# Seams between the first two layers of a four-layer image kernel: where the projection, the additions and a table load stand

## The chip, the cores and the metric

The kernel runs on one core of one Trainium2 chip. The core has five engines that matter here: TensorE (PE, matrix products, with its weight loads listed as PEld), VectorE (DVE), ScalarE (ACT), GpSimd (POOL) and SyncE (SP, which issues transfers). The metric is the device time of one execution in microseconds. All data is fp32.

## The reference

A batch of four images, 56 x 56 pixels with 128 channels, passes through four layers, each of the form `x = x + layer(groupnorm(x))`. The change touches layers 0 and 1 and the step between them:

```python
# layer 0: window attention, then full attention, then an MLP
xf = windows(x)                                     # 7 x 7 windows, shifted by 3, 4 heads
xf = xf + mha(layernorm(xf))                        # all 3136 pixels, 4 heads of 32, ends with @ wo + bo
h  = gelu(layernorm(xf) @ w1 + b1)                  # 128 -> 512
xf = xf + (h @ w2 + b2)                             # 512 -> 128
x  = x + xf
# layer 1: every pair of pixels of one image row
x_n      = groupnorm(x)
edge     = relu(x_n @ W1.T [i] + x_n @ W2.T [j] + be)   # 56 x 56 pairs of each row
x        = x + relu(concat(x_n, edge.sum(j)) @ Wn.T + bn)
```

Layers 2 (spectral attention) and 3 (a convolution with sums along rows) follow for all images together; they are not changed.

## The kernel before

The four images go through layers 0 and 1 one after the other (`first_layers` in `build`). Channels lie on the 128 partitions and the 3136 pixels on the free axis, in window order until the end of layer 0 (`xw` is the input, `xf` the running result) and in image order from then on (`x1`). For one image the steps are:

1. `fast_windows`: group norm, window attention, and the layer norm and q, k, v of the full attention.
2. `fast_attention`: the 3136 queries are worked off in 7 blocks of 448 (`blk(j)`). For each block the scores of 24 chunks of 128 keys and one of 64 are computed (L639, four heads in four 32-row strips of the array), exponentiated by ACT into a ring of slots (L641), summed by DVE (`f_acc`, L594) and multiplied with the values (L600). Score tiles alternate between two PSUM areas `s0` and `s1` (four and three banks). A list `late` delays the value products by two turns and the closing step `finish` by three, so that they stand behind scores of the next block. `finish(j)` takes one of the two PSUM areas (`pd`), lets PE sum the exponentials over the partitions (L607, L610), takes the reciprocal on DVE (L612) and writes the normalised block to `oT` (L613). PE's order in this stage is the order of the program text; that of the other engines is a scheduler's.
3. The output projection: seven matmuls with `wo`, all in one PSUM tile `po`, each followed by an addition to `xf` on DVE (L663, L664).
4. `mlp`: eight parts of 392 pixels. For all eight parts, PE centres the part (`m_pc`, L670), ACT squares it and copies it, PE averages the squares, ACT takes the root (L682) and DVE the reciprocal (L683) and the product (L868). Then, part by part, four matmuls and four Gelus make the hidden layer (L855, L856), one part ahead, four matmuls make the result `m_po` (L876, two PSUM banks in turn), DVE adds it to `xf` (L877), POOL adds `xw` and writes image rows of `x1` in three pieces (L883, L885, L886; two times three for the last part, whose rows wrap around), and DVE takes the statistics of those rows (L887). PE's order is that of the text here too.
5. `edge_layer`: `group_norm_factors` (L2320 to L2332) makes mean and factor, seven norms write `xg` (L192), and each of seven blocks of eight image rows is projected twice (`e_pa` L922, `e_pc` L924), evacuated by ACT (`evacuate`), combined in 14 turns of four pixels by DVE (`e_td`, L967) or by POOL and ACT (`e_tp`, L969, L971), added up by PE in `e_acc` (L974), and brought to the result (`output`, `finish`). The orders of PE, ACT and DVE are those of the text here.

Of the kernel before, what the change touches and what calls it, by code (L numbers as in the profile page):

```python
# [11 lines left out]
F32 = mybir.dt.float32  # L12
AF = mybir.ActivationFunctionType
ALU = mybir.AluOpType
# [4 lines left out]
P = 128  # L19
# [20 lines left out]
def blk(j):  # L40
    return slice(j * NB, (j + 1) * NB)
# [149 lines left out]
def apply_norm(k, out, xt, mr):  # L191
    k.nc.vector.tensor_scalar(out, xt, mr[:, 0:1], mr[:, 1:2], ALU.subtract, ALU.mult)  # L192
# [367 lines left out]
def fast_attention(k, w, xw, xf, mr):  # L560

    nc, tc = k.nc, k.tc
    scale = 1.0 / math.sqrt(32.0)
    heads = [slice(32 * h, 32 * h + 32) for h in range(4)]
    half = (slice(0, 64), slice(64, 128))
    with ExitStack() as es:  # L570
        big = es.enter_context(tc.tile_pool(name="f_big", bufs=1))
        qT = big.tile([P, TOK], F32, name="f_qT")
        kT = big.tile([P, TOK], F32, name="f_kT")
        va = big.tile([P, 25, P], F32, name="f_va")
        fast_windows(k, w, xw, xf, mr, qT, kT, va)

        ring = es.enter_context(tc.tile_pool(name="f_ring", bufs=1)).tile([P, RING, NB], F32, name="f_ring")
        wk = es.enter_context(tc.tile_pool(name="f_wk", bufs=2))
        ps = es.enter_context(tc.tile_pool(name="f_ps", bufs=1, space=PSUM))
        oT = es.enter_context(tc.tile_pool(name="f_out", bufs=1)).tile([P, TOK], F32, name="f_oT")  # L580
        late = []
        n = 0

        def bank(turn):
            return ps.tile([P, (4, 3)[turn], 512], F32, tag="s%d" % turn, name="f_s%d" % turn)

        def slots(j, c):
            s = (96 * j + 4 * c) % RING
            return ring[:, s:s + 4, :]

        def sums(j, c, acc):

            if 0 < c < SUMMED:
                nc.vector.tensor_add(acc, slots(j, 0) if c == 1 else acc, slots(j, c))  # L594

        def values(j, c, po, p24):
            for h in range(4):
                o = half[h % 2] if c == 24 else slice(0, P)
                p = p24[o, h // 2, :] if c == 24 else slots(j, c)[:, h, :]
                nc.tensor.matmul(po[heads[h], :NB], va[o, c, heads[h]], p, start=(c == 0), stop=(c == 24))  # L600

        def finish(j, raw, acc, p24, pd):

            for c in range(SUMMED - 1, 24):
                p = acc if c < SUMMED else slots(j, c)
                for h in range(4):
                    nc.tensor.matmul(pd[heads[h], 0, :NB], k.ones[:, 0:32], p[:, h, :], start=(c < SUMMED), stop=False)  # L607
            for h in range(4):
                o = half[h % 2]
                nc.tensor.matmul(pd[heads[h], 0, :NB], k.ones[o, 0:32], p24[o, h // 2, :], start=False, stop=True)  # L610
            den = wk.tile([P, NB], F32, name="f_den")
            nc.vector.reciprocal(den, pd[:, 0, :NB])  # L612
            nc.vector.tensor_mul(oT[:, blk(j)], raw, den)  # L613

        def flush(all_=False):

            nonlocal n
            if n % 2 and not all_:
                return
            while late and (all_ or late[0][0] < n):  # L620
                _, f, *a = late.pop(0)
                if f is finish:
                    a.append(bank(n % 2))
                    n += 1
                f(*a)

        with tc.manual_schedule(engines={mybir.EngineType.PE}):
            for j in range(NBLK):
                po = ps.tile([P, 512], F32, tag="po", name="f_po")
                raw = wk.tile([P, NB], F32, name="f_raw")  # L630
                acc = wk.tile([P, 4, NB], F32, name="f_acc")
                t, done = 0, 0
                while t < 96:
                    turn, slot = n % 2, (96 * j + t) % RING
                    m = min((4, 3)[turn], RING - slot, 96 - t)
                    ss = bank(turn)
                    for i in range(m):
                        c, h = divmod(t + i, 4)
                        nc.tensor.matmul(ss[:, i, :NB], kT[heads[h], c * P:(c + 1) * P], qT[heads[h], blk(j)],  # L639
                                         start=True, stop=True)  # L640
                    nc.scalar.activation(ring[:, slot:slot + m, :], ss[:, :m, :NB], AF.Exp, scale=scale)  # L641
                    t += m
                    while 4 * (done + 1) <= t:
                        sums(j, done, acc)
                        late.append((n + 2, values, j, done, po, None))
                        done += 1
                    n += 1
                    flush()
                ss = bank(n % 2)
                for h in range(4):  # L650
                    nc.tensor.matmul(ss[half[h % 2], h // 2, :NB], kT[heads[h], 24 * P:TOK], qT[heads[h], blk(j)],
                                     start=True, stop=True)
                p24 = wk.tile([P, 2, NB], F32, name="f_p24")
                nc.scalar.activation(p24, ss[:, 0:2, :NB], AF.Exp, scale=scale)
                late.append((n + 2, values, j, 24, po, p24))
                late.append((n + 2, nc.scalar.copy, raw, po[:, :NB]))
                late.append((n + 3, finish, j, raw, acc, p24))
                n += 1
                flush()
            flush(True)  # L660
        for j in range(NBLK):
            pm = ps.tile([P, 512], F32, tag="po", name="f_pf")
            nc.tensor.matmul(pm[:, :NB], w.wo, oT[:, blk(j)], start=True, stop=True)  # L663
            nc.vector.scalar_tensor_tensor(xf[:, blk(j)], pm[:, :NB], w.fbvo, xf[:, blk(j)], ALU.add, ALU.add)  # L664


def centre(k, pool, centred, src, squares, j):
# [171 lines left out]
def mlp(k, w, xf, xw, x1, st):  # L839
# [4 lines left out]
    with ExitStack() as es:  # L844
# [25 lines left out]
        for wi, ts in enumerate(parts):  # L870
            hT = ahead
            if wi < 7:
                ahead = hidden(parts[wi + 1])
            po = psum.tile([P, 512], F32, tag="acc", name="m_po")
            for f in range(4):
                nc.tensor.matmul(po[:, :N], w.w2[:, f, :], hT[:, f, :], start=(f == 0), stop=(f == 3))  # L876
            nc.vector.scalar_tensor_tensor(xf[:, ts], po[:, :N], w.b2, xf[:, ts], ALU.add, ALU.add)  # L877
            a = xf[:, ts].rearrange("p (w i j) -> p w i j", w=8, i=7)
            x = xw[:, ts].rearrange("p (w i j) -> p w i j", w=8, i=7)
            for i0, i1 in (((0, 7),) if wi < 7 else ((0, 4), (4, 7))):  # L880
                r0 = (7 * wi + 3 + i0) % HH
                rows = x1[:, r0:r0 + i1 - i0, :]
                nc.gpsimd.tensor_add(  # L883
                    rows[:, :, 3:52].rearrange("p i (w j) -> p w i j", w=7), a[:, 0:7, i0:i1, :], x[:, 0:7, i0:i1, :])
                nc.gpsimd.tensor_add(rows[:, :, 52:56], a[:, 7, i0:i1, 0:4], x[:, 7, i0:i1, 0:4])  # L885
                nc.gpsimd.tensor_add(rows[:, :, 0:3], a[:, 7, i0:i1, 4:7], x[:, 7, i0:i1, 4:7])  # L886
                nc.vector.bn_stats(st[:, wi + (i0 > 0), :], rows.rearrange("p l n -> p (l n)"))  # L887

# [3 lines left out]
def edge_layer(k, w, x1, st):  # L894
# [9 lines left out]
    with ExitStack() as es:  # L904
# [6 lines left out]

        mr = group_norm_factors(k, wk, bank, st)
        xg = big.tile([P, TOK], F32, name="e_xg")
        for j in range(NBLK):
            apply_norm(k, xg[:, blk(j)], xf[:, blk(j)], mr)
        ready = {}

        def project(j):
            if j >= NBLK:
                return  # L920
            pa = psum.tile([P, 512], F32, tag="pa", name="e_pa")
            nc.tensor.matmul(pa[:, :NB], w.W1, xg[:, blk(j)], start=True, stop=True)  # L922
            pc = psum.tile([P, 512], F32, tag="mm", name="e_pc")
            nc.tensor.matmul(pc[:, :NB], w.W2, xg[:, blk(j)], start=True, stop=True)  # L924
            ready[j] = pa, pc

        def evacuate(j):
# [21 lines left out]
            nc.vector.scalar_tensor_tensor(xf[:, blk(j)], po[:, :NB], w.nbn, xf[:, blk(j)], ALU.max, ALU.add)  # L949

        with tc.manual_schedule(engines={mybir.EngineType.PE, mybir.EngineType.Activation, mybir.EngineType.DVE}):
            for j in range(2):
                project(j)
                evacuate(j)
            last = None
            for j in range(NBLK):
# [4 lines left out]
                for g, e in enumerate(EDGE_TURNS):  # L961
# [18 lines left out]
                        evacuate(j + 1)  # L980
                    if g == 7 and last:
                        finish(last[0], po)
                    if g == 9:
                        nc.vector.tensor_reduce(rest, c[:, :, 0:nd], AX.X, ALU.add)
                sums = wk.tile([P, 4, NB], F32, name="e_sums")
# [1473 lines left out]
```

## Time and profile before

| What | Value |
|---|---|
| time, median of 3 runs | 3927.94 us (3925.56 to 3935.25) |
| span of the profiled execution | 3931.4 us |
| seven projections of the four images, PE (L663) | 56 passes, median 954 ns |
| additions on POOL (L883), four images | 36, median 907 ns |
| norms of layer 1 on DVE (L192, e_xg) | 28, median 505 ns |
| reciprocals of the layer norm in the MLP (L683), one image | 8, mean 2571 ns |

A line of the timeline gives the start, the duration, the engine, the source line and operation, the tile written and the tiles read with their shapes, and a count where equal instructions follow each other. The bracket says how long the engine stood idle before, and which instruction's end (engine, tile, line) ended that; "issue" means that no wait is visible. An fp32 matmul appears as two passes. Busy times of PE overlap, so a full PE is read from the absence of brackets rather than from its share.

### The profile page before, as it was taken

The page shows a single profiled execution, that of the slowest core. Times are in us where ns is not written, and L with a number is a line of the kernel's source. Part 1 is how long each engine was busy: PE and PEld are TensorE (multiplying, and loading weights), DVE is VectorE, ACT ScalarE, POOL GpSimd, SP SyncE. Part 2 cuts the span into 40 slices and gives each one's busy share as a digit, 9 for nine tenths or more (in the row PEclk, how much of TensorE's full clock was granted, in tenths as well). Part 3 has the DMA queues.
Part 4 walks back from the last instruction along what each step waited for, and adds up shares of the span by engine and source line. Part 5 has one row for each costly group of instructions (what it writes and reads, how often), then busy time and mean ns, then how long its engine had stood idle before and what let it go on. Part 6 is the DMA issues. An engine that isn't in the chain of part 4 may idle for free. (4 is left out here: it accounts for less than half of the span.)

```text
span 3931.4 us, 79382 instructions
## 1 busy us (share of the span) xinstructions
PE 3547.4 (90%) x35416; PEld 1589.8 (40%) x35416; DVE 2900.7 (74%) x2667; ACT 2048.0 (52%) x2055; POOL 1211.2 (31%) x671
## 2 busy tenths in 40 slices
PE   6899988989998898999889999998977979999988
PEld 4322234542223455222245532223446433336554
DVE  6588867758887685888769578885975867775664
ACT  4577754557775445877555467773522012215332
POOL 0000006600000570000047100001861869984665
PEclk8999999999999999999999999998978989999988
DMA  2000000000000000000000000000022048841101
GB/s 94 1 1 1 1 1 19 19 1 1 1 1 1 18 11 9 1 1 1 1 17 3 18 1 1 1 1 1 3 88 84 2 91 170 172 99 78 58 9 50
DMA packets 73497, 111.13 MB, mean 28 GB/s; under 512 B 62140, under 2 KB 63932, under 8 KB 67900
## 3 DMA queue, kind: packets, MB, share of 16 engines
q1 hardware_dynamic: 14460, 93.13, 7.9%
q10 hardware_dynamic: 58688, 12.85, 2.0%
q8 instruction: 280, 4.59, 0.5%
q14 instruction: 69, 0.57, 0.0%
HBM read 79.46 MB, written 26.51 MB: 27 GB/s over the span
## 5 line engine op out<-in xcount | busy, mean ns | idle before, releaser
L641 ACT ACTIVATE f_ring<-f_s 128x1792 f32<-128x1792 f32 (+3 forms) x796 | 1097.8, 1429 | 315.7 <-PE f_s L639 313.5
L594 DVE TENSOR_TENSOR f_acc<-f_acc,f_ring 128x1792 f32<-128x1792 f32 x560 | 1133.9, 2025 | 80.8 <-ACT f_ring L641 27.2
L639 PE MATMUL f_s<-f_qT,f_kT 32*128 32x448 f32 x5376 | 740.0, 572 | 57.7 <-ACT f_ring L641 26.7
L883 POOL TENSOR_TENSOR x<-xf,xw 128x343 f32<-128x343 f32 (+2 forms) x36 | 29.9, 831 | 2129.3 <-issue 2056.9
L600 PE MATMUL f_po<-f_ring,f_va 128*32 128x448 f32 x5376 | 591.3, 548 | 0.0
L967 DVE TENSOR_TENSOR e_td<-e_pa,e_c 128x1792 f32<-128x1792 f32 x252 | 491.2, 2012 | 8.0 <-ACT e_a L934 8.0
L969 POOL TENSOR_TENSOR e_tp<-e_a,e_c 128x1792 f32<-128x1792 f32 x140 | 451.7, 3258 | 143.6 <-PE e_acc L974 104.5
L639 PEld LDWEIGHTS f_s<-f_qT,f_kT 32*128 32x128 f32 x5376 | 268.3, 183 | 538.2 <-ACT f_ring L641 368.4
L974 PE MATMUL e_acc<-e_td,t_shared 32*32 32x448 f32 x8064 | 322.3, 545 | 25.5 <-DVE e_td L967 15.1
L971 ACT ACTIVATE e_tp<-e_tp 128x1792 f32<-128x1792 f32 x140 | 235.2, 1697 | 186.9 <-POOL e_tp L969 186.9
L1561 DVE TENSOR_TENSOR u_ud<-u_px,u_d 112x1792 f32<-112x1792 f32 x144 | 240.1, 1707 | 100.0 <-PE u_po L1566 86.3
L600 PEld LDWEIGHTS f_po<-f_ring,f_va 128*32 128x32 f32 x5376 | 133.0, 109 | 399.3 <-issue 398.3
L1566 PE MATMUL u_po<-u_ud,AT 112*64 112x448 f32 x960 | 202.2, 551 | 30.0 <-DVE u_ud L1561 30.0
L974 PE MATMUL e_acc<-e_tp,t_shared 32*32 32x448 f32 x4480 | 220.6, 544 | 2.5 <-ACT e_tp L971 2.3
L1563 POOL TENSOR_TENSOR u_up<-xh,u_d 112x1792 f32<-112x1792 f32 x64 | 193.8, 3054 | 32.8 <-PE u_po L1566 13.2
L974 PEld LDWEIGHTS e_acc<-e_td,t_shared 32*32 32x32 f32 x8064 | 133.6, 103 | 150.0 <-DVE e_td L967 60.2
L594 DVE TENSOR_TENSOR f_acc<-f_ring 128x1792 f32<-128x1792 f32 x28 | 56.7, 2024 | 105.3 <-ACT f_ring L641 76.4
L1566 PEld LDWEIGHTS u_po<-u_ud,AT 112*64 112x64 f32 x960 | 65.1, 138 | 154.9 <-issue 87.1
L1566 PE MATMUL u_po<-u_up,AT 112*64 112x448 f32 x576 | 125.3, 542 | 0.1
L1432 POOL TENSOR_TENSOR q_u<-iS,q_g 128x1792 f32<-128x1792 f32 x32 | 112.8, 3557 | 13.1 <-PE q_acc L1447 13.1
L974 PEld LDWEIGHTS e_acc<-e_tp,t_shared 32*32 32x32 f32 x4480 | 94.4, 103 | 54.7 <-ACT e_tp L971 18.6
L856 ACT ACTIVATE m_hT<-m_ph,w_fb 128x392 f32<-128x392 f32 x128 | 72.7, 589 | 73.6 <-PE m_ph L855 68.1
(459 smaller groups left out, 4747.4 us busy)
## 6 DMA issues: line engine op xcount, KB each, us to landing
u_d<-dd SPq DMA_DIRECT2D x48, 784.0 KB
xw<-in_x SPq DMA_DIRECT2D x4, 1568.0 KB
x2d<-x SPq DMA_DIRECT2D x4, 1568.0 KB
x_xs<-xad ACTq DMA_DIRECT2D x32, 196.0 KB
xm<-x_ev ACTq DMA_DIRECT2D x64, 98.0 KB
o_a<-xm SPq DMA_DIRECT2D x8, 784.0 KB
o_x<-x2d SPq DMA_DIRECT2D x4, 1568.0 KB
out<-o_o SPq DMA_DIRECT2D x12, 448.0 KB
```

What stands on the lines that cost most here:

```text
L594: nc.vector.tensor_add(acc, slots(j, 0) if c == 1 else acc, slots(j, c))
L600: nc.tensor.matmul(po[heads[h], :NB], va[o, c, heads[h]], p, start=(c == 0), stop=(c == 24))
L639: nc.tensor.matmul(ss[:, i, :NB], kT[heads[h], c * P:(c + 1) * P], qT[heads[h], blk(j)], start=True, stop=True)
L641: nc.scalar.activation(ring[:, slot:slot + m, :], ss[:, :m, :NB], AF.Exp, scale=scale)
L967: nc.vector.tensor_tensor(t, am, cm, ALU.max)
L969: nc.gpsimd.tensor_sub(t, bc(a.rearrange("p (l n) -> p l n", l=8), 1, 4), cm)
L971: nc.scalar.activation(tf, tf, AF.Relu)
L974: nc.tensor.matmul(acc[quarters[q], r, :NB], k.ident[o, o], t[o, q].rearrange("p l n -> p (l n)"), start=(g == 0), stop=(g == len(EDGE_TUR ...
L1432: nc.gpsimd.tensor_mul(u, bc(st.iS[:, bp, c, :HH], 1, HEADS), bc(g[:, n, c, :], 2, HH))
L1561: nc.vector.tensor_mul(u, bc(px[:, :, :NB], 2, m), dm)
L1563: nc.gpsimd.tensor_mul(u, bc(x, 2, m), dm)
L1566: nc.tensor.matmul(po[64 * b2:64 * b2 + 64, :NB], st.AT[:, 8 * i + h0 + q, 2 * bp + b2, :], u[:, b2, q, :], start=(left == 16), stop=(left ...
```

## The change

It moves work at two seams. (1) The output projection of block j - 1 is issued in `finish(j)`, ahead of block j's sums, into the second bank of the same PSUM area; only the last block's projection is left behind the attention. (2) In the MLP `xf + b2 + xw` is made on DVE ahead of time, and three additions on DVE take the MLP's result straight from PSUM and write the image rows; POOL has no part in it any more. (3) A root of one column is issued on ACT behind the last Gelu, so that the root's table is loaded before layer 1 asks for it. (4) In layer 1 only the norms of the first two blocks stay on DVE ahead of the edge tiles; those of blocks 2 to 6 go to ACT, two blocks ahead, as a scaled copy with a shift that is made once. (5) The projection that ACT evacuates first, `e_pc`, is issued first.

```diff
@@ fast_attention
         def finish(j, raw, acc, p24, pd):
+            if j:
+                project(j - 1, pd[:, 1, :NB])
             for c in range(SUMMED - 1, 24):
...
+        def project(j, pm):
+            nc.tensor.matmul(pm, w.wo, oT[:, blk(j)], start=True, stop=True)
+            nc.vector.scalar_tensor_tensor(xf[:, blk(j)], pm, w.fbvo, xf[:, blk(j)], ALU.add, ALU.add)
...
-        for j in range(NBLK):
-            pm = ps.tile([P, 512], F32, tag="po", name="f_pf")
-            nc.tensor.matmul(pm[:, :NB], w.wo, oT[:, blk(j)], start=True, stop=True)
-            nc.vector.scalar_tensor_tensor(xf[:, blk(j)], pm[:, :NB], w.fbvo, xf[:, blk(j)], ALU.add, ALU.add)
+        project(NBLK - 1, ps.tile([P, 512], F32, tag="po", name="f_pf")[:, :NB])
@@ mlp
-            nc.vector.scalar_tensor_tensor(xf[:, ts], po[:, :N], w.b2, xf[:, ts], ALU.add, ALU.add)
+            nc.vector.scalar_tensor_tensor(xf[:, ts], xf[:, ts], w.b2, xw[:, ts], ALU.add, ALU.add)
             a = xf[:, ts].rearrange("p (w i j) -> p w i j", w=8, i=7)
-            x = xw[:, ts].rearrange("p (w i j) -> p w i j", w=8, i=7)
+            x = po[:, :N].rearrange("p (w i j) -> p w i j", w=8, i=7)
...
-                nc.gpsimd.tensor_add(
+                nc.vector.tensor_add(
                     rows[:, :, 3:52].rearrange("p i (w j) -> p w i j", w=7), a[:, 0:7, i0:i1, :], x[:, 0:7, i0:i1, :])
-                nc.gpsimd.tensor_add(rows[:, :, 52:56], a[:, 7, i0:i1, 0:4], x[:, 7, i0:i1, 0:4])
-                nc.gpsimd.tensor_add(rows[:, :, 0:3], a[:, 7, i0:i1, 4:7], x[:, 7, i0:i1, 4:7])
+                nc.vector.tensor_add(rows[:, :, 52:56], a[:, 7, i0:i1, 0:4], x[:, 7, i0:i1, 0:4])
+                nc.vector.tensor_add(rows[:, :, 0:3], a[:, 7, i0:i1, 4:7], x[:, 7, i0:i1, 4:7])
...
+        nc.scalar.activation(wk.tile([P, 1], F32, name="m_root"), hT[:, 3, 0:1], AF.Sqrt, bias=k.eps, scale=0.0)
@@ edge_layer
-        for j in range(NBLK):
-            apply_norm(k, xg[:, blk(j)], xf[:, blk(j)], mr)
+        shift = wk.tile([P, 1], F32, name="e_shift", bufs=1)
+        nc.vector.tensor_scalar(shift, mr[:, 0:1], mr[:, 1:2], -1.0, ALU.mult, ALU.mult)
+        def normed(j):
+            if j < 2:
+                apply_norm(k, xg[:, blk(j)], xf[:, blk(j)], mr)
+            elif j < NBLK:
+                nc.scalar.activation(xg[:, blk(j)], xf[:, blk(j)], AF.Identity, bias=shift, scale=mr[:, 1:2])
...
         def project(j):
...
+            pc = psum.tile([P, 512], F32, tag="mm", name="e_pc")
+            nc.tensor.matmul(pc[:, :NB], w.W2, xg[:, blk(j)], start=True, stop=True)
             pa = psum.tile([P, 512], F32, tag="pa", name="e_pa")
             nc.tensor.matmul(pa[:, :NB], w.W1, xg[:, blk(j)], start=True, stop=True)
-            pc = psum.tile([P, 512], F32, tag="mm", name="e_pc")
-            nc.tensor.matmul(pc[:, :NB], w.W2, xg[:, blk(j)], start=True, stop=True)
...
+            for j in range(2):
+                normed(j)
             for j in range(2):
                 project(j)
                 evacuate(j)
...
+                    if g == 8:
+                        normed(j + 2)
```

The order of the instructions that the two programs give each engine shows where the scheduler put what is not written out. On DVE the addition of a projection stands in front of the reciprocal of the block whose `finish` issued it (in two of six blocks with a running sum of the next block between them). Four of the MLP's eight `xf + b2 + xw` stand ahead of the first layer-norm reciprocal, the others between the additions of the first three parts. On ACT the norm of block j + 2 stands behind the third `e_tp` of block j.

## The prediction

> **What bounds the kernel now.** I read the page's head and its busy row first, then the table of stretches for one image (image 0, 525 to 762 us), then the timeline of the seam that the change touches, then the waits. The stage is one image of layers 0 and 1, and there are four images in a row; the first output projections of images 0, 1 and 3 start at 525.6, 1235.3 and 2659.0 us, so a gain in one image counts four times.
>
> ```profile
> span 3931.4 us, 79382 instructions
> PE 3547.4 (90%) x35416; PEld 1589.8 (40%) x35416; DVE 2900.7 (74%) x2667; ACT 2048.0 (52%) x2055; POOL 1211.2 (31%) x671
> ...
> 525.00:545.00 20.00, 12.70 (x23) 3.61 (x16) 8.10 (x9) 0.00 (x0) 0.00 (x0) 0.64 0.00 0
> ...
> 558.00:601.00 43.00, 42.31 (x128) 23.64 (x126) 23.85 (x27) 19.79 (x34) 9.18 (x21) 1.00 0.00 1
> 601.00:613.00 12.00, 5.35 (x11) 2.98 (x12) 5.49 (x16) 2.56 (x5) 1.77 (x6) 0.72 0.37 136
> ```
>
> The last three rows are stretches: length, then busy time and count of PE, weight loads, DVE, ACT and POOL, then the PE clock and DMA. PE is the bound nearly everywhere (42.31 of 43 us in the MLP). The two exceptions are the seams: 525 to 545 (ACT at zero, PE clock 0.64) and 601 to 613 (no engine busy half the time). The change works on both. The first one in the timeline (start, duration, engine, line; in brackets the idle time before and who ended it):
>
> ```profile
> 522.36 0.96 PE L607 MATMUL f_s<-f_acc,c_ones 128*32 128x448 f32 x8 [1.52 <-DVE f_acc L594]
> ...
> 525.77 2.96 DVE L612 RECIPROCAL f_den<-f_s 128x448 f32<-128x448 f32 x1 [3.56 <-PE f_s L610]
> ...
> 529.15 0.62 DVE L613 TENSOR_TENSOR f_oT<-f_raw,f_den 128x448 f32<-128x448 f32 x1
> ...
> 541.65 1.86 PE L663 MATMUL f_pf<-f_oT,t_first 128*128 128x448 f32 x2 [0.78 <-DVE xf L664]
> 543.55 0.68 DVE L664 SCALAR_TENSOR_TENSOR xf<-f_pf,w_fbvo,xf 128x448 f32<-128x448 f32 x1 [1.96 <-PE f_pf L663]
> ...
> 544.29 2.98 PE L670 MATMUL m_pc<-xf,c_centre 128*128 128x392 f32 x4 [0.78 <-DVE xf L664]
> ```
>
> The reader sees a ping-pong over one PSUM bank: two passes of a projection, its evacuation, the next projection, every 2.64 us (541.65, before it 539.01), with nothing beside it. From the last reciprocal to the MLP's first matmul it takes 544.29 - 525.77 = 18.5 us. Within the attention, however, PE is full: in the 56 us from 370 to 426 it is busy 52.96.
>
> The second seam:
>
> ```profile
> 600.89 0.63 DVE L877 SCALAR_TENSOR_TENSOR xf<-m_po,t_first,xf 128x392 f32<-128x392 f32 x1
> 601.60 0.60 POOL L883 TENSOR_TENSOR x<-xf,xw 128x196 f32<-128x196 f32 x1 [1.32 <-DVE xf L877]
> ...
> 603.84 0.40 DVE L2320 BATCH_NORM_AGGREGATE gf_mv<-x_st 128x2 f32<-128x54 f32 x1
> ...
> 606.23 1.28 ACT L2331 ACT_TABLE_LOAD   x1 [10.02 <-PE e_mm L2330]
> 607.53 0.26 ACT L2331 ACTIVATE gf_t<-e_mm,c_eps 128x1 f32<-128x1 f32 x1
> ...
> 608.59 1.86 PE L922 MATMUL e_pa<-e_xg,t_edge 128*128 128x448 f32 x2 [2.44 <-DVE e_xg L192]
> ...
> 611.98 0.63 ACT L932 ACTIVATE e_c<-e_pc,e_nbe 128x448 f32<-128x448 f32 x1 [4.19 <-PE e_pc L924]
> ...
> 612.51 0.52 ACT L934 COPY e_a<-e_pa 128x448 f32<-128x448 f32 x1
> ...
> 613.07 13.61 DVE L967 TENSOR_TENSOR e_td<-e_pa,e_c 128x1792 f32<-128x1792 f32 x7 [2.00 <-ACT e_a L934]
> ```
>
> This is one serial chain: evacuate, add, statistics, two group matmuls, table load, root, norm, both projections, both evacuations, first edge tile.
>
> [...] the trace shows projections with 0.375 us between passes at 525.6 and double that later (1.86 for two at 541.65, 1.02 when fast). [...]
>
> **The change part by part, for one image.**
>
> *Seam of attention and MLP.* Six of seven projections leave the tail. What stays is reciprocal 2.96, product 0.62, one projection (two passes, 0.75 us apart in all at the fast clock, 1.5 at the slow one) and handovers of some 0.1: 4.4 to 5.2, taken as 4.8. The centring matmul of the first parts needs only early blocks, so it follows the projection without its evacuation. 18.5 - 4.8 = **-13.7**.
>
> *The projections inside the attention.* Each puts two passes at the head of a block's sums, in a stretch where PE is full: 2 x 0.375 = 0.75[...], 0.80. Five pay it. The sixth (block 5, in block 6's finish) falls into the 1.52 us in which PE waits for f_acc (522.36 above): nothing. Its 0.68 us evacuation stands before the reciprocal on DVE; it needs only the first matmul, and DVE idles 3.56 us there before the reciprocal, or in other seams the reciprocal is late by 0.68 together with the sums' 0.80, so the wait of PE for the bank (0.2 to 1.2 us per seam, on DVE f_den) stays as it is. Behind the evacuation on DVE are the reciprocal and the next block's running sums; PE waits for the reciprocal because the bank holds the sums. 5 x 0.80 = **+4.0** (bounds: 3.75, and 6 x 0.95 = 5.7).
>
> *MLP.* The scheduler puts four of the eight new additions (xf + b2 + xw) ahead of the first of the eight layer-norm reciprocals. The fourth overwrites part 3, so it waits for m_pc of part 3, whose second pass ends at about 550.1, and takes 0.6: the first reciprocal starts at 550.8, not 550.11, +0.7. PE does not see it until the third m_po, which needs the first m_po bank back; that wait is 0.54 now (574.25). After the reciprocals DVE frees the bank with three adds, not one evacuation of 0.57. The trace has no such add on DVE; the nearest row is the window stage's product of h1 with a PSUM tile of 392 elements, 0.56[...]; with 0.51, 0.18 and 0.18 I take 0.9, some 0.4 more. 0.7 + 0.4 = **+1.1** (bounds 0.3 and 2). Later parts have 5.3 us each on PE against 0.63 + 0.9 + 0.57 on DVE: hidden. POOL's adds leave and free nothing that waits.
>
> *End of the MLP.* From 600.89 to 603.84 it is 2.95. After: adds of 0.36, 0.17, 0.17, 0.31, 0.17, 0.17 and the two statistics of 0.39 and 0.34, 2.08: **-0.9** (0.4 to 1.3).
>
> *Edge start.* The root's table is loaded behind the last Gelu, while ACT idles 10 us: **-1.3**. A one-column e_shift goes before the first norm on DVE: **+0.2**. With e_pc before e_pa, e_c (0.63) runs during e_pa's passes, and e_td and POOL's e_tp wait for e_a alone: **-0.5**. Five norms of 0.44 each (3.05 for seven) leave DVE, which was waiting for ACT at that point anyway: nothing. On ACT they stand behind the block's third e_tp, where ACT idles (5.25 us before the e_tp of 649.09); nothing. The image load of xw can start some 25 us earlier, and was in no wait.
>
> Sum: -13.7 + 4.0 + 1.1 - 0.9 - 1.3 + 0.2 - 0.5 = -11.1 us an image, times four -44.4. Layers 2 and 3 are not touched and only shift. 3927.94 - 44.4 = 3883.5, given as **3884**.
>
> **The rivals.**
> 1. *The inserted projections are hidden altogether*, because PE waits on bank releases at each seam. For: those waits exist (0.34 to 1.23 us on f_den). Against: they come after the reciprocal, which shifts with the sums. Then -15.1 an image, -60, 3868.
> 2. *Each insertion costs double*: matmul 0.80 and evacuation 0.68 in series on the way to the reciprocal, with a bubble, 1.6 to 1.7, all six: +10, not 4. For: ACT idles 3.7 to 5.6 us at each seam, so the seam is a chain. Against: the evacuation runs beside 3 us of sums. Then -5.1 an image, -20, 3907.
> 3. *Slower*: the seam's chain loses the order of DVE, a reciprocal waits behind a running sum of 2.02 as well (0.80 + 0.68 + 2.02 = 3.5, six times +21), against -14.2 of the rest with the m_po wait at its upper bound of 2. +6.8 an image, +27, 3955. For: two seams in seven have a running sum queued ahead of the reciprocal. Against: DVE has that order before the change too.
>
> **How the numbers follow.** Forecast 0.65, rival 1 0.13, rival 2 0.18, rival 3 0.04. The bounds of the forecast's own terms: best -14.1 + 3.75 + 0.3 - 1.3 - 1.6 = -13.0, 3876; worst -13.3 + 5.7 + 2.0 - 0.4 - 1.6 = -7.6, 3898. The range takes rival 1 in, and the near part of rival 2, with 3 us for the spread of the times (3925.56 to 3935.25): 3865 to 3904. Faster by over 0.3% (11.8 us): the forecast, rival 1 and most of rival 2, 0.93; same 0.04, the far end of rival 2; slower 0.03.
>
> **What would show it.** Right: in image 0 the stretch from the last f_den reciprocal to m_pc is about 4.8 us; f_oT matmuls into f_s have 0.75 for two passes with the reciprocals not more than 0.8 later after the sums' start; each attention block is 0.8 longer; a wait of PE for the bank of m_po of some 1.6 us; the root without a table load before it and e_td 2.5 us sooner after the MLP's last matmul. Wrong: blocks longer by 1.5 us or more (rival 2), blocks of the old length (rival 1), waits of PE for m_po in more than one part, or e_pa/e_pc waiting for an ACT norm.

## The result and the profile after

The changed kernel takes 3964.87 us (median of 4 runs, 3962.67 to 3967.96); the kernel before, run beside it, 3931.6 us. The ratio is 1.0086, with a 95% interval of 1.0068 to 1.0104: slower by about 33 us, where 44 us less were forecast. The page of the changed kernel:

```profile
span 3963.8 us, 79391 instructions
PE 3571.9 (90%) x35416; PEld 1593.5 (40%) x35416; DVE 2913.9 (74%) x2759; ACT 2062.4 (52%) x2079; POOL 1167.5 (29%) x563
```

The busy row is nearly the one of before, so it can't tell where the time went. A table by stage can. It is read from the starts of a few DVE instructions that both kernels have (the f_den reciprocals, the statistics' aggregation gf_mv, the first e_td), for image 0:

| stretch of image 0, us | before | after | difference | predicted |
|---|---|---|---|---|
| first to last reciprocal f_den (attention) | 317.15 | 339.80 | +22.65 | +4.0 |
| last f_den to gf_mv (tail, MLP) | 78.07 | 65.66 | -12.41 | -13.5 |
| gf_mv to first e_td (edge start) | 9.23 | 7.34 | -1.89 | -1.6 |

Over four images the three rows give +86.7, -49.5 and -7.6, together +29.6 of the 32.4 by which the spans differ; layers 2 and 3, from the start of layer 1's last addition to the end of the span, took 1036.6 and 1033.4. So two rows came out nearly as forecast, and the first is wrong by a factor of five to six. From reciprocal to reciprocal the six blocks are longer by 1.8, 5.4, 4.7, 4.9, 5.0 and 0.8 us.

The second of these seams, before, in the timeline:

```profile
310.87 0.96 PE L607 MATMUL f_s<-f_acc,c_ones 128*32 128x448 f32 x8 [0.15 <-ACT f_ring L641]
311.65 1.69 PE L607 MATMUL f_s<-f_ring,c_ones 128*32 128x448 f32 x16
...
313.26 0.96 PE L610 MATMUL f_s<-f_p,c_ones 64*32 64x448 f32 x8
314.29 2.96 DVE L612 RECIPROCAL f_den<-f_s 128x448 f32<-128x448 f32 x1 [0.23 <-PE f_s L610]
```

and after:

```profile
315.95 1.02 PE L618 MATMUL f_s<-f_oT,t_first 128*128 128x448 f32 x2 [0.15 <-ACT f_ring L647]
317.11 2.03 DVE L594 TENSOR_TENSOR f_acc<-f_ring 128x1792 f32<-128x1792 f32 x1 [3.77 <-ACT f_ring L647]
319.05 0.68 DVE L619 SCALAR_TENSOR_TENSOR xf<-f_s,w_fbvo,xf 128x448 f32<-128x448 f32 x1
...
319.79 1.72 PE L609 MATMUL f_s<-f_acc,c_ones 128*32 128x448 f32 x8 [2.82 <-DVE xf L619]
321.28 2.57 PE L609 MATMUL f_s<-f_ring,c_ones 128*32 128x448 f32 x16
...
323.78 0.96 PE L612 MATMUL f_s<-f_p,c_ones 64*32 64x448 f32 x8
324.80 2.96 DVE L614 RECIPROCAL f_den<-f_s 128x448 f32<-128x448 f32 x1 [5.07 <-PE f_s L612]
```

Three things are to be seen. The sums (L609) now wait, not for the projection but for its *addition* on DVE (L619), though they read and write nothing that the addition touches: they lie in the first bank of `pd`, the projection in the second. The addition starts 3.10 us after the projection (1.06 in the first seam, shown next): it stands behind a running sum of the next block that started at 317.11 and takes 2.03. And after the wait of 2.82 us the sums are slower: 1.72 and 2.57 for the groups that took 0.96 and 1.69. The addition starts at 319.05, when the running sum that started at 317.11 is near its end (319.14).

The first seam has no running sum in that place:

```profile
259.48 1.02 PE L618 MATMUL f_s<-f_oT,t_first 128*128 128x448 f32 x2
260.54 0.68 DVE L619 SCALAR_TENSOR_TENSOR xf<-f_s,w_fbvo,xf 128x448 f32<-128x448 f32 x1 [1.94 <-PE f_s L618]
261.28 0.96 PE L609 MATMUL f_s<-f_acc,c_ones 128*32 128x448 f32 x8 [0.78 <-DVE xf L619]
262.06 1.69 PE L609 MATMUL f_s<-f_ring,c_ones 128*32 128x448 f32 x16
```

Here the wait is 0.78, the sums keep their speed, and the block costs 1.8 us more. The waits of the whole attention, and the PE clock at the two seams (column after the five engines):

```profile
PEld f_s L609 <- DVE xf L619: 14.4, 6, 3.5
PE f_s L609 <- DVE xf L619: 10.0, 6, 2.8
```

```profile
258.00:268.00 10.00, 7.99 (x68) 2.04 (x64) 4.48 (x4) 3.44 (x4) 0.00 (x0) 1.00 0.00 0
317.00:328.00 11.00, 7.87 (x58) 1.95 (x62) 5.71 (x4) 1.80 (x3) 0.00 (x0) 0.84 0.00 0
```

All six sums wait for L619, 10.0 us in all, up to 2.8 at once; in these two seams the clock is full where the wait was short and 0.84 where it was long. The long seam adds up: from the start of the projection to that of the sums it is 319.79 - 315.95 = 3.84 us that were not there before (0.95 for two passes, see the first experiment, and the wait), and the sums take 319.79 to 323.78 = 3.99 up to their last group (L612) where before it is 310.87 to 313.26 = 2.39, so 1.60 more. Together this is the 5.4 us. Over the six seams of image 0 the passes make 6 x 0.95 = 5.7, the waits 10.0 and the slower sums, in the four long seams, 1.60 + 1.65 + 2.25 + 2.25 = 7.8 us: 23.5, near the 22.65 of the table (in the sixth seam 1.5 us of wait, for f_acc, stood there before).

The wait comes in every image, the slow sums don't. The same seam in image 3:

```profile
2478.46 0.96 PE L609 MATMUL f_s<-f_acc,c_ones 128*32 128x448 f32 x8 [2.82 <-DVE xf L619]
2479.24 1.69 PE L609 MATMUL f_s<-f_ring,c_ones 128*32 128x448 f32 x16
```

After the same 2.82 us the sums keep their speed.

The tail:

```profile
551.71 2.96 DVE L614 RECIPROCAL f_den<-f_s 128x448 f32<-128x448 f32 x1 [3.47 <-PE f_s L612]
...
555.46 1.86 PE L618 MATMUL f_pf<-f_oT,t_first 128*128 128x448 f32 x2 [3.81 <-DVE f_oT L615]
...
557.35 0.68 DVE L619 SCALAR_TENSOR_TENSOR xf<-f_pf,w_fbvo,xf 128x448 f32<-128x448 f32 x1 [1.95 <-PE f_pf L618]
558.09 2.98 PE L673 MATMUL m_pc<-xf,c_centre 128*128 128x392 f32 x4 [0.78 <-DVE xf L619]
```

From the reciprocal to `m_pc` it is 6.4 us, not 4.8: the centring waits for the last block's addition, although its part lies in block 0. MLP end and edge start:

```profile
615.71 0.36 DVE L886 TENSOR_TENSOR x<-xf,m_po 128x196 f32<-128x196 f32 x1 [1.34 <-PE m_po L879]
...
617.37 0.40 DVE L2335 BATCH_NORM_AGGREGATE gf_mv<-x_st 128x2 f32<-128x54 f32 x1
...
619.57 0.26 ACT L2346 ACTIVATE gf_t<-e_mm,c_eps 128x1 f32<-128x1 f32 x1 [6.93 <-PE e_mm L2345]
...
624.14 0.53 ACT L945 COPY e_a<-e_pa 128x448 f32<-128x448 f32 x1 [0.86 <-PE e_pa L935]
...
624.71 3.96 DVE L980 TENSOR_TENSOR e_td<-e_pa,e_c 128x1792 f32<-128x1792 f32 x2 [3.59 <-ACT e_a L945]
```

The last result reaches gf_mv in 1.66 us after its first addition, the root has no table load in front of it, and `e_td` starts at the end of `e_a`, as forecast.

### The profile page after: what moved, and what is told of

The parts are those of the page before. It is cut to its first block, busy times and chain, and to the rows that moved or that the text cites. A ratio compares the mean times of both kernels' runs of the same rounds, so it can differ in the third digit from the quotient of the medians.

```text
span 3963.8 us, 79391 instructions
## 1 busy us (share of the span) xinstructions
PE 3571.9 (90%) x35416; PEld 1593.5 (40%) x35416; DVE 2913.9 (74%) x2759; ACT 2062.4 (52%) x2079; POOL 1167.5 (29%) x563
## 5 line engine op out<-in xcount | busy, mean ns | idle before, releaser
L614 DVE RECIPROCAL f_den<-f_s 128x448 f32<-128x448 f32 x28 | 82.8, 2958 | 100.3 <-PE f_s L612 100.3
```

## The experiments

The theory W, from this trace: the projection and the sums share one PSUM tile, and the program lets an instruction on it wait for all earlier ones on it whatever their bank. So the sums wait for the evacuation (10.0 us in image 0), the evacuation stands on DVE behind the running sum of 2.03 us, and behind the long wait the sums are slow (granted clock 0.84 there, 1.00 in the first seam). That the wait makes them slow was the author's guess. Rival R: the inserted work itself costs that much where PE is full. The tables below are for image 0 unless said otherwise; ratios are to the kernel before, run on the same chip; n_r is the layer norm's reciprocal in the MLP, and line numbers are each kernel's own.

| kernel | time, us | ratio (95%) | first to last f_den | last f_den to first n_r | n_r to gf_mv | gf_mv to e_td |
|---|---|---|---|---|---|---|
| before | | 1 | 317.15 | 24.34 | 53.73 | 9.23 |
| the change | 3964.87 | 1.0086 (1.0068 to 1.0104) | 339.80 | 13.11 | 52.55 | 7.34 |
| 1 addition after the sums | 3922.89 | 0.9963 (0.9953 to 0.9974) | 324.51 | 12.60 | 52.55 | 7.35 |
| 2 own PSUM tile | 3913.79 | 0.9946 (0.9926 to 0.9965) | 323.91 | 12.91 | 52.54 | 7.35 |
| 3 only the projections | 3956.17 | 1.0043 (1.0029 to 1.0057) | 337.51 | 12.21 | 53.72 | 9.23 |
| 4 only the rest | 3940.43 | 1.0001 (0.9987 to 1.0016) | 317.15 | 19.34 | 52.55 | 7.35 |
| 5 evacuation on ACT | 3930.19 | 0.9981 (0.9971 to 0.9991) | 326.53 | 13.09 | 52.55 | 7.35 |
| 6 other bank, same tile | 3964.16 | 1.0071 (1.0047 to 1.0096) | 337.63 | 12.84 | 52.54 | 7.35 |
| 7 last one in the MLP | 3925.17 | 0.9973 (0.9963 to 0.9984) | 323.93 | 10.87 | 58.32 | 7.56 |
| 8 as 7, without the rest | 3925.65 | 0.9980 (0.9969 to 0.9991) | 323.92 | 7.63 | 60.50 | 9.23 |
| 9 last one early in the MLP | 3905.50 | 0.9922 (0.9898 to 0.9946) | 323.95 | 10.02 | 52.55 | 7.55 |
| 10 as 9, without the rest | 3905.34 | 0.9922 (0.9900 to 0.9944) | 323.93 | 9.89 | 53.72 | 9.12 |
| 12 only the rest, again | 3935.53 | 1.0002 (0.9990 to 1.0015) | 317.15 | 25.22 | 54.25 | 7.55 |

The kernel before took 3931.60 us beside the change, 3937.29 beside 1 to 4, 3934.51 beside 5 to 8 and 3934.52 beside 9 to 12.

**1. The addition behind the sums.** The projection stays where the change puts it; only the addition is emitted later.

```diff
+            if j:
+                add_on(j - 1, pd[:, 1, :NB])
             den = wk.tile([P, NB], F32, name="f_den")
...
         def project(j, pm):
             nc.tensor.matmul(pm, w.wo, oT[:, blk(j)], start=True, stop=True)
+
+        def add_on(j, pm):
             nc.vector.scalar_tensor_tensor(xf[:, blk(j)], pm, w.fbvo, xf[:, blk(j)], ALU.add, ALU.add)
```

> Theory W (wait): in the changed kernel the sums of a block wait for the evacuation of the projection, because both lie in one PSUM tile[...]. Here the projection's matmul stays where it is and only its addition is issued behind the sums, so nothing of PE's work changes and the sums wait for nothing new. W expects no wait of the sums on xf, the sums at the fast clock, an attention (first to last f_den reciprocal, image 0) of 325 to 327 us against 339.8 with the change and 317.2 before it (0.75 for the matmul and 0.68 for the addition, which now stands between the sums and the reciprocal, six times), and 3905 to 3918 us in all. Rival R (the inserted work itself, a matmul of another shape and one more DVE operation in the seam, is what costs): as with the change, 338 to 341 us and 3962 to 3968.

Its timeline at the second seam:

```profile
318.36 1.02 PE L620 MATMUL f_s<-f_oT,t_first 128*128 128x448 f32 x2 [0.15 <-ACT f_ring L651]
319.31 0.96 PE L609 MATMUL f_s<-f_acc,c_ones 128*32 128x448 f32 x8
320.08 1.69 PE L609 MATMUL f_s<-f_ring,c_ones 128*32 128x448 f32 x16
...
322.73 0.68 DVE L623 SCALAR_TENSOR_TENSOR xf<-f_s,w_fbvo,xf 128x448 f32<-128x448 f32 x1 [1.18 <-PE f_s L612]
323.33 2.95 DVE L616 RECIPROCAL f_den<-f_s 128x448 f32<-128x448 f32 x1
```

The same matmuls in the same place now cost 0.95 us, the sums follow without a wait and at full speed, and the attention is 324.51, just under the 325 to 327 of W and far from the 338 to 341 of R. R falls. The total of 3922.89 is over W's 3905 to 3918; beside a kernel before of 3937.29 it is a gain of 14 us. The price has only moved: the addition now waits for the sums (for their last group, L612, not for the projection, which ended 3 us earlier), and the reciprocal is later by it.

**2. A PSUM tile of its own.** The projection goes into the `po` bank, behind the first ring group of the sums, when ACT has emptied that bank.

```diff
-            if j:
-                project(j - 1, pd[:, 1, :NB])
...
+                if c == SUMMED and j:
+                    project(j - 1, ps.tile([P, 512], F32, tag="po", name="f_pf")[:, :NB])
...
+            if c == 0:
+                pos[j] = ps.tile([P, 512], F32, tag="po", name="f_po")
```

> The projection of block j - 1 goes into the bank of the value products, which is free between the copy of block j and the first value product of block j + 1, in the middle of block j's sums. Neither the sums nor the score tiles share a tile with it, so only the 0.75 us of its two passes should be left. W expects an attention of 321 to 323 us (six times 0.75 to 0.9 more than 317.2), a shorter seam to the MLP too if the first centring matmul no longer waits for the last addition (5 us instead of 6.4), and 3883 to 3896 us in all. R expects 338 us or more and 3955 or more; a third possibility, that the value products of the next block wait for the addition in its bank, would show as a new wait of f_po on xf and lie between, 3900 to 3930.

```profile
313.27 0.94 PE L615 MATMUL f_s<-f_ring,c_ones 128*32 128x448 f32 x8
314.14 1.02 PE L626 MATMUL f_pf<-f_oT,t_first 128*128 128x448 f32 x2
315.09 0.96 PE L615 MATMUL f_s<-f_ring,c_ones 128*32 128x448 f32 x8
...
315.60 0.68 DVE L627 SCALAR_TENSOR_TENSOR xf<-f_pf,w_fbvo,xf 128x448 f32<-128x448 f32 x1
317.00 2.96 DVE L622 RECIPROCAL f_den<-f_s 128x448 f32<-128x448 f32 x1 [0.72 <-PE f_s L620]
```

In this timeline the addition runs beside the sums, as the prediction had it, and the sums have no wait left. (Value products of a next block wait twice for an addition in their bank, the third possibility of the expectation, but for 0.7 us of the image in all.) The attention, 323.91 for 321 to 323 expected, is 6.76 us longer than before, 1.13 a projection where 0.80 was predicted: 0.95 from the start of the two passes to the next sums, and a sixth that is not free. The expected total was missed: it is 23.5 us under the kernel before, where 36 to 49 would have met it (from the 3931.6 beside the change). Part of it is the tail, where the last addition still holds up the centring (6.4, not the expected 5); part lies in layers 2 and 3 (1042.8 us; see 11).

**3 and 4. The parts alone.** In 3 the MLP and the edge layer are those of before; in 4 the attention is.

> The kernel before with the projection's part of the change alone. W: the attention is lengthened by the same 21 to 23 us an image and the tail shortened by the same 12.1, so 3931.6 + 4 x (21.7 - 12.1) = 3970, and 3966 to 3975 with the rest of the change missing, which is worth 2 us an image. If the rest of the change cost something, this would be faster than the change's 3964.9.

> The changed kernel with the projection put back behind the attention. W: only the MLP and the edge layer's start differ from before, 2.0 to 2.5 us an image, so 3921 to 3925. If the rest of the change has a part in the loss: 3932 or more.

The projections alone are slower (1.0043), with all six waits of the sums for the addition, but less so than was expected: 3956.17 for 3966 to 3975. It is also under the change's 3964.9, the sign that was named for a cost of the rest. The stages of the rest show none: from the last f_den to e_td it takes 1.3 to 2.2 us an image longer here than with the change. What is shorter is the attention, 1340.9 us in the four images for 1356.7, after the same waits: 9 seams have slow sums here, 15 there, and these add 14.5 us in the four images here, 27.5 there. The granted clock was 0.955 to 0.958 in all executions of 3, 0.949 to 0.951 in those of the change. Why it differs stays open.

The rest alone is no gain in the total: 3940.43, ratio 1.0001, where 3921 to 3925 was expected (0.997 to 0.998 of the 3931.6). Yet gf_mv to e_td is 1.9 shorter. The 19.34 of its tail in the table is no gain of the rest either, as this code is that of before: in images 0 and 1 the seven projections run at full speed (1.02 us for two passes instead of 1.86) after the same waits as before, and in images 2 and 3 the stretch is 25.2 and 24.8. In the same profile layers 2 and 3 take 1049.6 us, 13 longer than before; 12 takes this up.

**5. The evacuation on ACT.** Same tile, same place, but DVE is out of the way.

```diff
-            nc.vector.scalar_tensor_tensor(xf[:, blk(j)], pm, w.fbvo, xf[:, blk(j)], ALU.add, ALU.add)
...
+                nc.scalar.activation(pj, pm, AF.Identity, bias=w.fbvo)
+                nc.gpsimd.tensor_add(xf[:, blk(j)], xf[:, blk(j)], pj)
```

> The changed kernel with the projection where the change puts it and in the same PSUM tile as the sums, but its evacuation on ScalarE (with the bias, into SBUF) and the addition to the residual on GpSimd. The sums still wait for the evacuation of their tile; only the place in VectorE's queue behind the 2.02 us running sum is gone. Theory W (shared tile, and the running sum ahead of the addition makes the wait long[...]): every seam costs what the one without a running sum ahead cost in the changed kernel, about +1.8 us; first to last reciprocal of an image 326 to 330 us (317.2 before, 338 to 340 changed), ratio to the kernel before 0.996 to 1.000. Rival Q (any wait at that place costs what is seen, VectorE's queue has no part): 337 to 341, ratio 1.006 to 1.010. Rival S (ScalarE's queue delays it and the next exponentials as much): 331 to 336, ratio about 1.003.

```profile
316.28 2.03 DVE L594 TENSOR_TENSOR f_acc<-f_ring 128x1792 f32<-128x1792 f32 x1 [4.12 <-ACT f_ring L652]
316.55 0.66 ACT L623 ACTIVATE f_pj<-f_s,w_fbvo 128x448 f32<-128x448 f32 x1
317.26 0.96 PE L609 MATMUL f_s<-f_acc,c_ones 128*32 128x448 f32 x8 [1.12 <-ACT f_pj L623]
...
318.04 1.69 PE L609 MATMUL f_s<-f_ring,c_ones 128*32 128x448 f32 x16
```

This takes the seam apart. The running sum is there as in the change, at the same point, but the evacuation passes it on another engine: the sums still wait, 1.12 us for `f_pj`, and then run at full speed. The attention is 326.53 (326.5 to 329.5 in the four images; in images 1 and 3 one seam each has slow sums, after a wait of 0.78). So what the shared tile costs beyond an own one, with the evacuation on ACT, is 326.5 - 323.9 = 2.6 us in image 0, and DVE's queue together with the slow sums 339.8 - 326.5 = 13.3: the waits are 10.0 there and 5.2 here, so 4.8, and the slow sums were 7.8.

**6. Another bank of the same tile**, `pd[:, 2, :NB]` for `pd[:, 1, :NB]`.

> The changed kernel with the projection in the third bank of the sums' PSUM tile and not in the second; nothing else. Theory T (what is waited for is the tile, whichever bank): nothing changes; first to last reciprocal 337 to 341 us, sums wait for the addition in every seam, ratio 1.007 to 1.010. Rival B (the bank beside the sums' matters): 322 to 326, ratio 0.994 to 0.997.

The attention is 337.6 and the sums wait six times for the addition, 10.0 us in all, the same as with the change. It is the tile and not the neighbouring bank. (Its time is that of two executions, 3959.41 and 3968.91 us.)

**7 to 10. A last projection that doesn't hold up the MLP.** With the own tile of 2, the last block's projection leaves the attention's pool and is made inside the MLP, in a bank of `m_po`; 7 puts it behind the centring of the fourth part, 9 behind that of the first. The last block's normalised values get an SBUF tile of their own (`f_oTl`). 8 and 10 are the same without the rest of the change.

```diff
-        project(NBLK - 1, ps.tile([P, 512], F32, tag="po", name="f_pf")[:, :NB])
+        k.rest = lambda pm: project(NBLK - 1, pm)
@@ mlp (9: first part; in 7 the condition is wi == 3, behind the layer norm of the part before)
                 centre(k, wk, pc[:, :N], xf[:, parts[wi]], squares, wi)
+                if not wi and k.rest:
+                    k.rest(psum.tile([P, 512], F32, tag="acc", name="f_pf")[:, :NB])
+                    k.rest = None
```

> The kernel with the projection in a PSUM tile of its own, and the last block's projection put into the MLP, behind the centring of its fourth part (a PSUM tile of the MLP's pool). Theory H (the first centring matmul waits for the last addition only because the attention's PSUM tiles are handed over whole): it now follows the last product at once, last reciprocal to first layer-norm reciprocal 9.4 to 10.2 us (12.6 to 13.3 with the projection in the tail), total 10 to 14 us less than with the projection in its own tile, ratio to the kernel before 0.990 to 0.993. Rival X (it waits for the addition because both touch the residual tile): the wait stays, 12.5 or more, and MLP centring would deadlock on nothing but come late, ratio 0.994 to 0.997. First to last reciprocal as with the own tile, 323.9.

> The same projections as in the last kernel (own PSUM tile, last one inside the MLP), but MLP result and edge start as in the kernel before. Tells what the rest of the change is worth in the total. By the stages of the trace (MLP end and edge start 3.1 us an image less, first layer-norm reciprocal up to 1 later): 8 to 12 us slower than the last kernel, ratio to the kernel before 0.993 to 0.996. By the total of the rest alone (1.0001): no difference from the last kernel within 4 us.

The timeline of 7:

```profile
547.07 0.92 PE L629 MATMUL f_pf<-f_oTl,t_first 128*128 128x448 f32 x2
547.16 5.06 DVE L697 RECIPROCAL n_r<-n_r 128x392 f32<-128x392 f32 x2
...
547.82 0.82 PE L684 MATMUL m_pc<-xf,c_centre 128*128 128x392 f32 x2
...
549.14 0.82 PE L684 MATMUL m_pc<-xf,c_centre 128*128 128x392 f32 x2
...
553.02 2.59 DVE L697 RECIPROCAL n_r<-n_r 128x392 f32<-128x392 f32 x1
555.54 0.58 DVE L630 SCALAR_TENSOR_TENSOR xf<-f_pf,w_fbvo,xf 128x448 f32<-128x448 f32 x1
...
556.17 1.67 PE L684 MATMUL m_pc<-xf,c_centre 128*128 128x392 f32 x2 [5.56 <-DVE xf L630]
```

Theory H was right on the first centring, which comes at once after the last reciprocal (first n_r at 9.2 to 10.9 in the four images, 12.6 to 13.3 in 2), but the total missed its band (0.9973 for 0.990 to 0.993): the addition now stands on DVE behind three layer-norm reciprocals, and the seventh centring, which does need block 6, waits 5.56 us for it. Rival X falls too: the centring of the fifth and sixth parts, which stands behind that addition in the program and reads the same residual tile, starts at 547.82 and 549.14, ahead of the addition. The 5.56 us are the mistake of the change once more, in another place. n_r to gf_mv shows it: 58.32 for 52.54. 8 comes out within the intervals of 7, so here too the rest is worth nothing that the total shows.

> As the kernel with the last projection inside the MLP, but behind the first part's centring instead of the fourth's, so that its addition stands on VectorE ahead of the layer-norm reciprocals and not behind three of them. Theory H2 (the 5.6 us wait of the seventh centring matmul was VectorE's queue): the wait goes; last to first layer-norm reciprocal 9.2 to 11 us, from there to the statistics 52.5 to 54.3 (58 to 59 with the late place), total 15 to 25 us under that kernel and below the one with only the own tile, ratio to the kernel before 0.990 to 0.994. Rival: a wait elsewhere takes its place, ratio 0.996 to 0.998.

> The same projections, with MLP result and edge start as in the kernel before. If the rest of the change is worth the 3 us an image less at MLP end and edge start that the traces show, less the first layer-norm reciprocal's 1 us: 8 to 12 us slower than the last kernel, ratio 0.9925 to 0.9965. If it is worth nothing: the same within 4 us.

The timeline of 9:

```profile
534.76 2.96 DVE L625 RECIPROCAL f_den<-f_s 128x448 f32<-128x448 f32 x1 [1.12 <-PE f_s L623]
537.77 1.67 PE L684 MATMUL m_pc<-xf,c_centre 128*128 128x392 f32 x2 [3.08 <-DVE f_den L625]
...
539.24 1.67 PE L629 MATMUL f_pf<-f_oTl,t_first 128*128 128x448 f32 x2
...
540.94 0.68 DVE L630 SCALAR_TENSOR_TENSOR xf<-f_pf,w_fbvo,xf 128x448 f32<-128x448 f32 x1 [0.83 <-PE f_pf L629]
```

H2 holds. The centring starts 3.0 us after the start of the last reciprocal (18.5 before, 6.4 with the change), the addition is done ahead of the layer-norm reciprocals, and the wait is gone. The centring now waits for the reciprocal, which reads the tile of the sums; with the change it waited for the addition, which reads `po`. No one bank explains both; a pool that is handed over whole does, though which bank `m_pc` gets is not shown here. 9 and 10 are the best versions of this study, at 0.9922: 29 us better than before and about 64 better than the change (1.0086 - 0.9922, of 3930). That they are alike says that the rest of the change adds nothing that the total shows.

**11 and 12. The kernel before and the rest, once more.**

> The kernel before, unchanged, profiled once more. If the spread of layers 2 and 3 (1033 to 1050 us in profiles of kernels that are alike there) is one of executions, its time there may lie anywhere in that band while layers 0 and 1 stay within 1 us an image; if it is a thing of each program, it is 1036 again.

> The kernel with everything of the change but the projections, once more, with more rounds, since its total (1.0001) did not show the 9 us that its stages did. Stages right: 0.997 to 0.9985. Stages given back elsewhere in a lasting way: 0.9995 to 1.0005, with layers 2 and 3 again near 1050 us in the profile.

Before, profiled again, has layers 0 and 1 within 0.5 us of the first profile in the stretches of the table, and layers 2 and 3 at 1033.6 (1036.6 the first time). The rest again has a ratio of 1.0002, so the 9 us of the expectation are not there; what came is its second branch, stages given back elsewhere. In this profile edge starts are 1.6 to 1.9 shorter than in 11, but the first n_r comes 0.9 to 2.0 later, n_r to gf_mv is 54.25 in three of four images (52.55 in the fourth, 53.73 before), and layers 2 and 3 take 1046.5.

Layers 2 and 3 took 1043 to 1050 us in the profiles of 1, 2, 4, 5, 7, 9 and 12, which all have the rest, and of 3, which hasn't; 1033 to 1037 in both of before, in 8 and 10 without the rest, and also in the change and in 6. In 9 against 10 it is plain: last f_den to e_td is 2.1 to 4.2 us an image shorter, layers 2 and 3 are 9.1 longer. The extra time is slower matmuls: the same 6608 passes keep PE busy for 896 to 905 us in the long profiles and 884 to 892 in the short ones, at a granted clock of 0.88 to 0.90 and 0.90 to 0.91. Why the clock is lower there isn't settled.

## Why the prediction was wrong, step by step

- **The failing step** is in the projections inside the attention: "Its 0.68 us evacuation stands before the reciprocal on DVE; it needs only the first matmul, and DVE idles 3.56 us there before the reciprocal ... so the wait of PE for the bank ... stays as it is." What the evacuation needs was asked, not what needs the evacuation. The sums do, because they share its tile (1 and 5 change only who waits for it or where it runs, and 6 shows that it is not the bank). And the queue behind and ahead of it was read for the reciprocal alone: a 2.03 us running sum stands ahead of it in four of six seams of image 0, the wait is 1.6 to 2.8 there, and in these four the sums take 1.60 to 2.25 us more than the 2.39 of before. (The paragraph on the order of the instructions names the running sums behind the addition, in two of six blocks, and not those ahead of it.) +22.65 instead of +4.0, of which the waits are 10.0 and the slow sums 7.8. The waits are shown (1, 2, 5, 6); that the slow sums come of them is likely from how often they follow, not shown for each seam.
- The two passes were priced at 0.80 (0.05 of it beside the passes, which no run shows) and cost 0.95 on PE, 1.13 with what follows (2). The profile before had it: the two passes at 525.64 start 0.48 us apart (0.91 in the slow ones), not 0.375, which is the distance in a longer run of like passes (L944). The sixth cost 0.8 in the change and 1.7 in 2 (49.72 to 51.42), not nothing. Without the wait the term would have been +6.8, above its bound of 5.7 but still a small miss.
- The tail was mis-sized: 4.8 predicted, 6.4 measured, since `m_pc` "needs only early blocks" by its data, but waited for the last addition. In 7 and 9, with the last projection in another pool, the same centring waits only for the last reciprocal, as it would if the attention's PSUM pool is handed over whole. The prediction's own extract had it: `m_pc` waits for "DVE xf L664" there too.
- MLP and edge start were right: PE waits 1.6 once for the bank of `m_po` (1.6 said), gf_mv to e_td is 1.89 shorter (1.6 said), the first n_r late by 0.9 (0.7 said). No row of before shows the DVE adds that were priced; after, three of one part take 0.51, 0.18 and 0.17 (592.02 to 592.71 with overlap: 0.69, where 0.9 was taken), the six of the last 0.36, 0.16, 0.16, 0.30, 0.15 and 0.16, and `e_shift` 0.21 (620.06). That they don't show in a total (4, 12; 7 against 8, 9 against 10) was not foreseen.
- Rival 3 had the sign and nearly the size, 3.5 a seam and +21 an image, and was given 4 in 100. Its sum is close to the 3.84 us from the projection to the sums in the long seam, but its mechanism was only in part the one that came: the additions, not the reciprocals, stand behind the running sum, and part of the 5 us of a seam is the slow sums (1.60 to 2.25). It was set aside because "DVE has that order before the change too", which is true of the order but not of who waits for it.

## What to carry to other kernels

Before putting new work into a bank that lies idle, ask which tile it belongs to: here the waits follow the tile, so an evacuation in one bank held up the matmuls in the next, and the first matmul of the next stage waited for whatever ended last in the pool before it (6.4 us after the start of the last reciprocal with the last projection in that pool, 3.0 without, in 9). For each added instruction list both what stands ahead of it on its engine and who waits behind it; a projection with a 0.68 us addition cost about 5 us a seam, slow sums included, where a 2 us operation stood ahead of the addition. If work is to fill a gap, give it its own tile and a place where its evacuation precedes the long operations, as in 9. And a gain of 2 us in a stage is not yet a gain in the total (9 is 2.1 to 4.2 us an image shorter than 10 from the last f_den to e_td, and both are at 0.9922): read both.

## What the runs showed of the hardware that was not expected

Slow sums often followed a wait of PE, but no length of wait decided it. With the change 16 seams of the four images have a running sum ahead of the addition and waits of 1.6 to 2.8 us; in 15 of them the sums are slow (2.39 us to their last group becomes 3.5 to 4.6). The eight seams with waits of 0.8 to 1.1 have no running sum there and no slow sums. But in the sixteenth a wait of 2.82 leaves the sums at full speed, in 3 only 9 of the same 16 seams are slow after the same waits, and in 5 two of 24 are slow, both after 0.78. What decides it isn't shown: no run changed the clock alone.
